# Layer 0 of a four-layer hybrid: the transposed delta comes back from memory, carries and delta u are done for a pair of scans at once, row and column sums are added in memory

## The chip, the cores and the metric

One Trainium2 chip, and of it one core. The time is device microseconds of that core for one execution of the whole program: four layers in a row, of which the change touches only the first. Names used below: PE is TensorE, DVE VectorE, ACT ScalarE, POOL GpSimd, SP the engine whose queue issues most of the DMAs.

## What is computed

Layer 0 is a selective state-space model run over images of 64 x 64 tokens in four scanning orders, with 256 channels and 16 states per channel. There are four images. Cut to what matters:

```
xc, z = split(x @ w_in);  xa = silu(conv3x3(xc) + conv_b)          # depthwise
dts, Bp, Cp = split(xa @ w_xproj);  delta = softplus(dts @ w_dt + b_dt)
xs = [xa by rows, xa by columns, both of these backwards]           # 4 orders
for each order, token i in that order:                              # delta, B, C always by rows
    h[d, n] = h[d, n] * exp(delta[d, i] * A[d, n]) + delta[d, i] * xs[d, i] * B[n, i]
    y[d, i] = sum over n of h[d, n] * C[n, i]
y = the four y put back in row order and added, + 4 * D * xa        # D is added once per order
out = layernorm(y) * silu(z) @ w_out
```

Only xs differs between the four orders; delta, B and C are those of the row order for all of them, so that the decay exp(delta A) is shared.

## The kernel before

**Tiling.** A unit is one image b and one half h of the 256 channels, so there are 8 units. A unit is cut in 64 chunks c of 64 tokens, which makes N = 512 iterations I of one loop. In an iteration the state tile `st` holds, for each of the 4 orders u, 128 partitions (64 channels x 2 halves of the states) by 16 x 64 elements. Orders are taken in two pairs, kp = 0 (u = 0, 1) and kp = 1 (u = 2, 3). Below, a *turn* is the work of one pair in one iteration; there are 1024 turns.

**A turn.** `products` (line 637) makes delta * u * B for two orders with eight matmuls of 64 x 64 x 512 on PE. Each order's result fills one `db` tile of two PSUM banks. The pool of `db` has three buffers, that is six banks, and a turn takes two of them. `scan` then does, for each order, an addition of the carry of the chunk before into the first column of each state (line 650) and the scan itself over 1024 elements (line 653), both on DVE. POOL makes the next carry (line 661) and multiplies the states of the pair by C in place (line 669). `total` sums over the states with matmuls against a stack of two identities (line 682), half of the states per call, into `yp`, and ACT copies the four results to `yr` and `yc`, which hold the row sums and the column sums of a whole unit (line 701). In the later half of the chunks the sums that stand there already are added first by four matmuls with the identity (line 694).

**Delta times u.** The scan's input wants delta with tokens on the partitions. `start` has ACT turn a chunk of delta round (line 599), `delta` transposes it and its mirror image on PE into `pt2` (line 617), and `inputs` multiplies it with the two tiles of u, `xo`, in two DVE operations (line 628). `yp` and `pt2` are halves of one PSUM tile, `aux`, which fills one bank.

**Work beside the loop.** Two steps of a generator run in each iteration, one after each turn: in the h = 0 units `back` (layer norm and output of the image before) and `front` (group norm and w_in of the image after) or, for the first image, `also` (tables for layer 1); in the h = 1 units `middle` (convolution, B, C and delta of the image after). What is left of the steps at chunk 59 of an h = 1 unit is run there at once. This work has one PSUM bank of its own, `bg`. `front` and `middle` of the first image run before the loop and take their banks from the `db` pool (`turn_bank`).

**What sets the order.** Inside the loop PE, DVE and ACT execute in the order in which the Python code records the instructions. POOL and SP are ordered by a scheduler. [...]a wait is a semaphore that another engine raises when an instruction is finished. Which waits are needed is worked out by the framework from the tiles that an instruction reads and writes. The loop body, cut to the calls:

```
nxt = start(I + 1); diagonal(nxt)
bs = products(now, 0); scan(I, now, 0, ...)
total(I - 2, 1); next(beside)
bs = products(now, 1); delta(nxt); inputs(nxt); scan(I, now, 1, ...)
next(beside); total(I - 1, 0)
```

Of the kernel before, what the change touches and what calls it, by code (L numbers as in the profile page):

```python
# [14 lines left out]
P = 128  # L15
# [144 lines left out]
def layer0(cm, x, W, x1, also, kept):  # L160
# [5 lines left out]
    with ExitStack() as ctx:  # L166
# [4 lines left out]
        t4 = ctx.enter_context(tc.tile_pool(name="l0t4", bufs=4))  # L171
        p2 = ctx.enter_context(tc.tile_pool(name="l0p2", bufs=2))
        db = ctx.enter_context(tc.tile_pool(name="l0db", bufs=3, space=PSUM))
# [31 lines left out]

        both = tl(wp, [P, TC], "both")
# [26 lines left out]


        yr = tl(wp, [P, S], "yr")
        yc = tl(wp, [P, S], "yc")

        aux = tl(pp, [P, 2, 2, P], "aux")
        yp = aux[:, 0].rearrange("p k (j t) -> p k j t", t=TC)
        pt2 = aux[:, 1]  # L240
# [19 lines left out]
        def begin(b):  # L260
            img[b] = {
                "zs": tl(dr, [P, 2, S], "zs"),
                "dl": tl(dr, [2, P, S], "dl_d"),
                "ct": tl(dr, [NST, S], "ct_d"),
                "xT": tl(dr, [2, S, P], "xT_d"),
                "y0": tl(dr, [P, 2, S], "y0_d"),
                "yr": tl(dr, [P, 2, S], "yr_d"),
            }
# [77 lines left out]
        def shifted(i, pool, tag):  # L346

            k, h = divmod(i, 2)
            x3 = tl(pool, [3 * CG, 4, 8 * PADW], tag, bufs=None if tag == "big" else 1)
            for dy in range(3):  # L350
                s0 = (8 * k + dy) * PADW
                nc.sync.dma_start(
                    x3[dy * CG : (dy + 1) * CG],
                    xc_d[4 * h : 4 * h + 4, :, s0 : s0 + 8 * PADW].rearrange("g p s -> p g s"),
                )
            return x3

        def middle(b, bank, pool, tag, ahead):

            ready = [shifted(i, pool, tag) for i in range(ahead)]  # L360
            for k in range(NBLK):
                cols = slice(k * BLK, (k + 1) * BLK)
                xa = []
                for h in range(2):
                    ps = bank()
                    x3 = ready.pop(0)
                    for dx in range(3):
                        for g in range(4):
                            nc.tensor.matmul(
                                ps[g * CG : (g + 1) * CG, :], lhsT=cdiag[:, 4 * h + g, dx, :],  # L370
                                rhs=x3[:, g, 0 : 8 * PADW].rearrange(
                                    "p (r w) -> p r w", w=PADW
                                )[:, :, dx : dx + HW],
                                start=(dx == 0), stop=(dx == 2),
                            )
                    if 2 * k + h + ahead < 2 * NBLK:
                        ready.append(shifted(2 * k + h + ahead, pool, tag))
                    xh = tl(tmp, [P, BLK], "t2k")
                    nc.scalar.activation(xh, ps, AF.Silu, bias=vec[:, 0, h : h + 1])
                    y0 = tl(tmp, [P, BLK], "t2k")  # L380
                    nc.scalar.activation(y0, xh, AF.Copy, scale=d4[:, h : h + 1])
                    nc.sync.dma_start(img[b]["y0"][:, h, cols], y0)
                    xa.append(xh)
                    yield
                    ps = bank()
                    for i in range(4):
                        nc.tensor.transpose(
                            ps[:, i * P : (i + 1) * P], xa[h][:, i * P : (i + 1) * P], cm.ident
                        )
                    t = tl(tmp, [P, 4, P], "t2k")  # L390
                    nc.scalar.copy(t, ps.rearrange("p (t c) -> p t c", c=P))
                    nc.sync.dma_start(
                        img[b]["xT"][h, cols, :].rearrange("(t p) c -> p t c", p=P), t
                    )
                    yield
                    if h == 0:
                        yield
                        yield
# [49 lines left out]
                yield  # L448
# [82 lines left out]
        def load(q):  # L531
# [3 lines left out]
            dl = tl(p2, [P, QC * TC], "dl")  # L535
            nc.sync.dma_start(dl, img[b]["dl"][h, :, cols])
# [6 lines left out]
            return {"dl": dl, "dp": dp, "dA": dA[q % 2], "h": h}  # L543
# [21 lines left out]
        def fetch(I):  # L565
# [9 lines left out]
            xo = tl(p2, [P, 2, P], "xo", bufs=3)  # L575
            xT = img[b]["xT"][h]
# [12 lines left out]
            inp[I] = {"ct": ct, "xo": xo, "dg": dg}  # L589
# [4 lines left out]
        def start(I):  # L594
            b, h, c = place(I)
            q = {"c": c, "h": h, "w": quads[I // QC], **inp.pop(I)}
            dlc = q["w"]["dl"][:, c % QC * TC : (c % QC + 1) * TC]
            dlr = tl(p2, [P, TC], "dlr")
            nc.scalar.copy(dlr, dlc[:, ::-1])
            q["dl"] = dlc, dlr  # L600
            return q
# [11 lines left out]
        def delta(q):  # L613

            pt = pt2[:, q["c"] % 2]
            for j in range(2):
                nc.tensor.matmul(  # L617
                    pt[j * TC : (j + 1) * TC, :], lhsT=q["dl"][j], rhs=cm.ident,
                    start=True, stop=True,
                )  # L620
            q["pt"] = pt

        def inputs(q):

            q["du"] = []
            for kp in range(2):
                d_ = tl(p2, [P, P], f"du{kp}")
                nc.vector.tensor_tensor(d_, q["xo"][:, kp, :], q["pt"], ALU.mult)  # L628
                q["du"].append(d_)

        def products(q, kp):
            bs = [tl(db, [P, 2 * NH0, TC], "db") for _ in range(2)]
            for g in range(2):
                for j in range(2):
                    half = slice(j * TC, (j + 1) * TC)
                    for p in range(2):
                        nc.tensor.matmul(  # L637
                            bs[j][p * TC : (p + 1) * TC, g * NH0 : (g + 1) * NH0, :],
                            lhsT=q["du"][kp][half, g * TC : (g + 1) * TC],
                            rhs=q["dg"][half, p * NH0 : (p + 1) * NH0, :],  # L640
                            start=True, stop=True,
                        )
            return bs

        def scan(I, q, kp, bs, st, old, new):
            c = q["c"]
            for j in range(2):
                u = 2 * kp + j
                if c:
                    nc.vector.tensor_tensor(  # L650
                        bs[j][:, :, 0], bs[j][:, :, 0], old[:, u, :], ALU.add
                    )
                nc.vector.tensor_tensor_scan(  # L653
                    st[:, u].rearrange("p n t -> p (n t)"),
                    q["w"]["dA"][:, c % QC].rearrange("p g n t -> p (g n t)"),
                    bs[j].rearrange("p n t -> p (n t)"),
                    0.0, ALU.mult, ALU.add,
                )
            us = slice(2 * kp, 2 * kp + 2)
# [16 lines left out]
        def total(I, part):  # L676
            b, h, c = place(I)
            st = states[I]
            late = c >= NCHUNK // 2
            for n in range(4 * part, 4 * part + 4):  # L680
                for p in range(2):
                    nc.tensor.matmul(  # L682
                        yp[p * TC : (p + 1) * TC], lhsT=both,
                        rhs=st[:, :, p * NH0 + n, :], start=(n == 0),
                        stop=(n == NH0 - 1 and not late),
# [3 lines left out]
            vs = [views(yc if kp else yr, c)[2 * j + kp] for j in range(2) for kp in range(2)]  # L689
            for j in range(2 if late else 0):  # L690

                for kp in range(2):
                    v = vs[2 * j + kp]
                    nc.tensor.matmul(  # L694
                        yp[:, kp, j, :], lhsT=cm.ident, rhs=v[:, ::-1] if j else v,
                        start=False, stop=(j + kp == 2),
                    )
# [5 lines left out]
            if late and c % 8 == 7:  # L703
                for r in (c - 7, NCHUNK - 1 - c):
                    rows = slice(r * TC, (r + 8) * TC)
                    nc.sync.dma_start(img[b]["yr"][:, h, rows], yr[:, rows])
            if c == NCHUNK - 1:
                for r in range(2):
                    rows = slice(r * S // 2, (r + 1) * S // 2)
                    nc.gpsimd.dma_start(  # L710
                        img[b]["y0"][:, h, rows], yc[:, rows], accum_op=ALU.add
                    )

        def turn_bank():
            return tl(db, [P, BLK], "db")
# [8 lines left out]
        for _ in run(front(0, turn_bank), middle(0, turn_bank, big, "big", 2)):  # L724
            pass
        N = 2 * B * NCHUNK
        states, quads, inp = {}, {0: load(0), 1: load(1)}, {}
# [9 lines left out]
        delta(nxt)  # L737
# [10 lines left out]
        with tc.manual_schedule(engines=engines):  # L748
            for I in range(N):
                b, h, c = place(I)  # L750
                clock[0] = I
                if h == 0 and c == 4:
                    gens = [back(b - 1, own_bank) if b else also(
                        tl(p2, [P, 4, 8 * PADW], "x3", bufs=1)[:, 0, 0 : 4 * C], tmp, t4, own_bank
                    )]
                    if b + 1 < B:
                        gens += [
                            front(b + 1, own_bank), wait(I - c + NCHUNK),
                            middle(b + 1, own_bank, p2, "x3", 1),
# [20 lines left out]
                bs = products(now, 0)  # L780
                scan(I, now, 0, bs, st, carry, new)
                if I > 1:
                    total(I - 2, 1)
# [9 lines left out]
                bs = products(now, 1)  # L793
                if nxt:
                    delta(nxt)
                    inputs(nxt)
                scan(I, now, 1, bs, st, carry, new)
                if beside:
                    next(beside, None)
                if I:  # L800
                    total(I - 1, 0)
                carry = new
            total(N - 2, 1)
            total(N - 1, 0)
            total(N - 1, 1)
# [4 lines left out]
def spectra(cm, W, cst, sp_d, room, tmp, t4, bank):  # L810

    nc = cm.nc
    kern = room.rearrange("p (a c) -> p a c", c=C)
# [1504 lines left out]
```

## Time and profile before

| what | value |
|---|---|
| median of 3 executions | 11008.79 us (10986.12 to 11056.8) |
| the profiled execution | 10974.05 us, span 10972.3 us |
| mean granted TensorE clock | 0.898 |
| before the loop (first scan starts) | 281.7 us |
| the loop, first scan to last | 281.7 to 6370.9 us, 6089 us, 11.9 us per iteration |
| its busiest engines, us busy in the loop | PE 5445.6, DVE 5422.5, POOL 5073.8, ACT 3063.3 |

The rest of the span, from 6371 us on, is layers 1 to 3. In the lists, a line such as L653 is line 653 of the kernel before; a group is all instructions of one line and shape, with its busy time, the mean of one in ns, and the idle time of its engine just before. PE's matmuls of 32-bit floats appear as two records each.

### The profile page before, as it was taken

The numbers are of one execution on the slowest core, as the hardware profiler recorded it, in microseconds if no ns is written. First come the engines' busy times: TensorE is split into PE (matmuls) and PEld (weight loads), VectorE is DVE, ScalarE is ACT, GpSimd is POOL, SyncE is SP. The second block draws the span as 40 slices with busy tenths as digits, with TensorE's granted clock in tenths as the row PEclk, the third lists the DMA queues.
The fourth block names the chain that finished last, engine by engine and source line by source line (L and its number), as shares of the span: only waits on it lengthen the run. The fifth ranks groups of instructions, "written<-read, shape, count | busy, mean of one in ns | idle before, by whom it ended". The sixth has DMA issues, their size and how long they took to land. (4 is left out here: it accounts for less than half of the span.)

```text
span 10972.3 us, 163387 instructions
## 1 busy us (share of the span) xinstructions
PE 9474.1 (86%) x59368; PEld 4529.1 (41%) x59368; DVE 7569.2 (69%) x11174; ACT 5425.1 (49%) x13536; POOL 5331.9 (49%) x2581
## 2 busy tenths in 40 slices
PE   6789998889998899998889954999999956988886
PEld 2344444344443344443344432444444434544442
DVE  1898988888988898988899966545452122355546
ACT  6666543555544564545542223777776622433321
POOL 0788888878888888887889940000000000000000
PEclk7899999999999899998999977999999976677777
DMA  5334443334443334443333341111100065022101
GB/s 147 106 107 149 131 128 114 109 109 149 136 132 116 107 117 151 135 122 113 109 106 99 103 120 36 41 35 35 39 24 17 16 191 104 17 46 56 37 24 46
DMA packets 1471160, 1009.46 MB, mean 92 GB/s; under 512 B 697540, under 2 KB 1296296, under 8 KB 1466008
## 3 DMA queue, kind: packets, MB, share of 16 engines
q1 hardware_dynamic: 1468056, 982.24, 30.3%
q0 software_dynamic: 2304, 16.78, 0.7%
q8 instruction: 475, 7.78, 0.3%
q14 instruction: 325, 2.66, 0.1%
HBM read 667.01 MB, written 331.61 MB: 91 GB/s over the span
## 5 line engine op out<-in xcount | busy, mean ns | idle before, releaser
L653 DVE TENSOR_TENSOR_SCAN big<-dA,db 128x1024 f32<-128x1024 f32 x2048 | 4680.0, 2286 | 82.1 <-ACT dA L560 3.2
L669 POOL TENSOR_TENSOR big<-big,ct 128x2048 f32<-128x2048 f32 x1024 | 4646.1, 4537 | 85.0 <-DVE big L653 5.4
L637 PE MATMUL db<-dg,du 64*64 64x512 f32 x16384 | 2442.7, 617 | 101.1 <-DVE db L650 87.8
L682 PE MATMUL aux<-big,both 128*64 128x256 f32 x16384 | 2104.0, 401 | 407.1 <-DVE db L650 260.6
L682 PEld LDWEIGHTS aux<-big,both 128*64 128x64 f32 x16384 | 1202.8, 142 | 1396.1 <-issue 622.9
L701 ACT COPY yr<-aux 128x64 f32<-128x64 f32 x1024 | 226.6, 222 | 2668.6 <-PE aux L694 1250.7
L637 PEld LDWEIGHTS db<-dg,du 64*64 64x64 f32 x16384 | 748.2, 135 | 1321.2 <-issue 1218.4
L608 ACT ACTIVATE dg<-mask,BT 128x64 f32<-128x64 f32 x4096 | 1007.4, 341 | 4.0 <-DMA dg_d<-dg 4.0
L1441 PE MATMUL av<-e,x 128*128 128x512 f32 x2048 | 974.0, 592 | 4.6 <-ACT e L1436 4.6
L1392 PE MATMUL qk<-a,xT 128*128 128x512 f32 x2048 | 966.6, 594 | 8.6 <-ACT e L1396 7.8
L1396 ACT ACTIVATE e<-qk,nk 128x512 f32<-128x512 f32 x1024 | 692.9, 685 | 539.2 <-PE qk L1392 538.4
L560 ACT ACTIVATE dA<-dp,A 128x252 f32<-128x252 f32 x2048 | 870.5, 509 | 1.4
L971 POOL TENSOR_TENSOR g_rs<-g_rs,qrow 128x4 f32<-128x4 f32 x32 | 41.1, 1285 | 1499.9 <-DVE g_rs L970 1499.9
L661 POOL TENSOR_TENSOR cy<-big,a 128x32 f32<-128x32 f32 x1008 | 272.8, 271 | 821.7 <-DVE big L653 524.4
L1392 PEld LDWEIGHTS qk<-a,xT 128*128 128x128 f32 x2048 | 378.0, 190 | 462.3 <-issue 358.0
L1441 PEld LDWEIGHTS av<-e,x 128*128 128x128 f32 x2048 | 381.6, 190 | 434.7 <-issue 393.6
L1436 ACT ACTIVATE e<-e 128x1024 f32<-128x1024 f32 x510 | 538.7, 1056 | 15.3
L1917 ACT ACTIVATE e<-s 72x576 f32<-72x576 f32 x448 | 273.3, 642 | 492.0 <-PE s L1910 489.0
L628 DVE TENSOR_TENSOR du<-xo,aux 128x128 f32<-128x128 f32 x1024 | 248.2, 284 | 379.5 <-PE aux L617 286.2
L650 DVE TENSOR_TENSOR db<-db,cy 128x16 f32<-128x16 f32 x2016 | 336.9, 167 | 202.0 <-PE db L637 184.2
L1928 POOL COPY vp<-vt 72x160 f32<-72x160 f32 x56 | 19.6, 352 | 890.8 <-PE po L1934 874.4
L2150 DVE SCALAR_TENSOR_TENSOR tex<-x,gw,tex 128x128 f32<-128x128 f32 x768 | 264.5, 344 | 256.1 <-PE x L2144 241.2
(525 smaller groups left out, 10869.4 us busy)
## 6 DMA issues: line engine op xcount, KB each, us to landing
ct<-ct_d SPq DMA_DIRECT2D x1024, 128.0 KB
dg_d<-dg SPq DMA_DIRECT2D x256, 512.0 KB
dg<-dg_d SPq DMA_DIRECT2D x256, 512.0 KB
xo<-xT_d SPq DMA_DIRECT2D x2048, 32.0 KB
x<-xc_d SPq DMA_DIRECT2D x144, 264.0 KB
dp<-dl_d SPq DMA_DIRECT2D x256, 128.0 KB
t2k<-in_x SPq DMA_DIRECT2D x96, 256.0 KB
sp<-sp_d SPq DMA_DIRECT2D x16, 1280.0 KB
```

The lines of the kernel that those rows point to most:

```text
L560: nc.scalar.activation(w["dA"][:, :, g, n, 1:], w["dp"][:, g, :, 1:], AF.Exp, scale=A[:, w["h"], g, n : n + 1],)
L608: nc.scalar.activation(q["dg"][:, n, :], mask, AF.Copy, scale=BT[:, q["c"], n : n + 1])
L637: nc.tensor.matmul(bs[j][p * TC : (p + 1) * TC, g * NH0 : (g + 1) * NH0, :], lhsT=q["du"][kp][half, g * TC : (g + 1) * TC], rhs=q["dg"][ha ...
L650: nc.vector.tensor_tensor(bs[j][:, :, 0], bs[j][:, :, 0], old[:, u, :], ALU.add)
L653: nc.vector.tensor_tensor_scan(st[:, u].rearrange("p n t -> p (n t)"), q["w"]["dA"][:, c % QC].rearrange("p g n t -> p (g n t)"), bs[j].re ...
L669: nc.gpsimd.tensor_tensor(sv, sv, q["ct"].rearrange("p n t -> p (n t)").unsqueeze(1) .to_broadcast([P, 4, NH0 * TC]), ALU.mult,)
L682: nc.tensor.matmul(yp[p * TC : (p + 1) * TC], lhsT=both, rhs=st[:, :, p * NH0 + n, :], start=(n == 0), stop=(n == NH0 - 1 and not late),)
L1392: nc.tensor.matmul(ps, lhsT=me["xT"][:, kt * P : (kt + 1) * P], rhs=me["a"][k], start=True, stop=True,)
L1396: nc.scalar.activation(e[:, j, :], ps, AF.Exp, bias=me["nk"][:, kt : kt + 1], scale=2.0)
L1436: nc.scalar.activation(es[g + 2], es[g + 2], AF.Exp)
L1441: nc.tensor.matmul(avs[b, k], lhsT=img[b]["x"][:, kt, :], rhs=e[:, j, :], start=(kt == 0), stop=(kt == NT - 1),)
L1917: nc.scalar.activation(e.rearrange("p j h q -> p j (h q)"), ss[p][0:HALF, :, 0 : 2 * WIN], AF.Exp, scale=0.5,)
```

## The change

- Delta is stored transposed too: `middle` transposes it, copies it, mirrors it by one matmul with a matrix `flip`, and writes both to `dT` in memory. `fetch` loads a chunk of it as `dt`. `delta`, the mirrored copy in `start`, and the loads of `dl` are gone. `inputs` is one operation on 128 x 256 elements instead of two on 128 x 128.
- `db` is no longer a pool of three tiles but one tile of three slots. `turns` lists which two slots a turn takes and in which order they are scanned. The carries of both orders are added by one operation, ahead of both scans. `turn_bank` gives slices of the same tile.
- The row sums of eight chunks and the column sums of half a unit are kept in pairs of small tiles `ys`. The later half is added to the earlier by DMAs that accumulate in memory, issued by POOL, instead of by matmuls.
- Both parts of `total` come one step later: part 0 of I - 2 after the first turn, part 1 of I - 2 after the second.
- `middle` has 15 steps per block of 512 tokens instead of 12; the loads of `shifted` are split in two, and use the tiles of `back`.

The diff, cut to its core:

```diff
-        db = ctx.enter_context(tc.tile_pool(name="l0db", bufs=3, space=PSUM))
+        db = tl(pp, [P, 3, 2 * NH0, TC], "db")
-        yr = tl(wp, [P, S], "yr")
-        yc = tl(wp, [P, S], "yc")
-        aux = tl(pp, [P, 2, 2, P], "aux")
-        yp = aux[:, 0].rearrange("p k (j t) -> p k j t", t=TC)
-        pt2 = aux[:, 1]
+        yp = tl(pp, [P, 2, 2, TC], "yp")
...
         (middle)
-                    if h == 0:
-                        yield
-                        yield
...
                     nc.sync.dma_start(img[b]["dl"][h, :, cols], r)
-                yield
+                    yield
+                    ps = bank()
+                    for i in range(4):
+                        nc.tensor.transpose(
+                            ps[:, i * P : (i + 1) * P], r[:, i * P : (i + 1) * P], cm.ident
+                        )
+                    for j in range(2):
+                        t = tl(tmp, [P, 4, P], "t2k")
+                        nc.scalar.copy(t, ps.rearrange("p (t c) -> p t c", c=P))
+                        nc.sync.dma_start(
+                            img[b]["dT"][h, j, cols, :].rearrange("(t p) c -> p t c", p=P), t
+                        )
+                        yield
+                        if j == 0:
+                            ps = bank()
+                            nc.tensor.matmul(
+                                ps, lhsT=flip, rhs=t.rearrange("p t c -> p (t c)"),
+                                start=True, stop=True,
+                            )
...
         (fetch)
+            dt = tl(p2, [P, P], "dt", bufs=3)
+            nc.sync.dma_start(dt[0:TC], img[b]["dT"][h, 0, c * TC : (c + 1) * TC, :])
+            nc.sync.dma_start(dt[TC:P], img[b]["dT"][h, 1, c * TC : (c + 1) * TC, :])
...
         def inputs(q):
-            for kp in range(2):
-                d_ = tl(p2, [P, P], f"du{kp}")
-                nc.vector.tensor_tensor(d_, q["xo"][:, kp, :], q["pt"], ALU.mult)
+            q["du"] = tl(p2, [P, 2, P], "du")
+            nc.vector.tensor_tensor(
+                q["du"], q["xo"], q["dt"].unsqueeze(1).to_broadcast([P, 2, P]), ALU.mult
+            )
+        turns = (
+            ({0: 0, 1: 1}, (0, 1), db[:, 0:2]), ({0: 0, 1: 2}, (1, 0), db[:, 0::2]),
+            ({0: 1, 1: 2}, (0, 1), db[:, 1:3]),
+        )
-        def products(q, kp):
-            bs = [tl(db, [P, 2 * NH0, TC], "db") for _ in range(2)]
+        def products(q, kp, turn):
+            bs = turn[0]
...
-                            bs[j][p * TC : (p + 1) * TC, g * NH0 : (g + 1) * NH0, :],
+                            db[p * TC : (p + 1) * TC, bs[j], g * NH0 : (g + 1) * NH0, :],
...
         (scan)
-            for j in range(2):
-                u = 2 * kp + j
-                if c:
-                    nc.vector.tensor_tensor(
-                        bs[j][:, :, 0], bs[j][:, :, 0], old[:, u, :], ALU.add
-                    )
+            if c:
+                nc.vector.tensor_tensor(
+                    turn[2][:, :, :, 0], turn[2][:, :, :, 0], old[:, us, :], ALU.add
+                )
+            for j in turn[1]:
                 nc.vector.tensor_tensor_scan(
...
         (total)
-            for j in range(2 if late else 0):
-                for kp in range(2):
-                    v = vs[2 * j + kp]
-                    nc.tensor.matmul(
-                        yp[:, kp, j, :], lhsT=cm.ident, rhs=v[:, ::-1] if j else v,
-                        start=False, stop=(j + kp == 2),
-                    )
...
+            if r == 7:
+                for i, r0 in enumerate((c - 7, NCHUNK - 1 - c)):
+                    to = img[b]["yr"][:, h, r0 * TC : (r0 + 8) * TC]
+                    if c < NCHUNK // 2:
+                        nc.sync.dma_start(to, ys[i])
+                    else:
+                        nc.gpsimd.dma_start(to, ys[i], accum_op=ALU.add)
+            if c % (NCHUNK // 2) == NCHUNK // 2 - 1:
                 for r in range(2):
                     nc.gpsimd.dma_start(img[b]["y0"][:, h, rows], ..., accum_op=ALU.add)
+        banks = [0]
         def turn_bank():
-            return tl(db, [P, BLK], "db")
+            banks[0] += 1
+            return db.rearrange("p u n t -> p (u n t)")[
+                :, banks[0] % 6 * BLK : (banks[0] % 6 + 1) * BLK
+            ]
...
-                bs = products(now, 0)
-                scan(I, now, 0, bs, st, carry, new)
+                turn = turns[2 * I % 3]
+                products(now, 0, turn)
+                scan(I, now, 0, turn, st, carry, new)
                 if I > 1:
-                    total(I - 2, 1)
+                    total(I - 2, 0)
...
-                bs = products(now, 1)
+                turn = turns[(2 * I + 1) % 3]
+                products(now, 1, turn)
                 if nxt:
-                    delta(nxt)
                     inputs(nxt)
-                scan(I, now, 1, bs, st, carry, new)
+                scan(I, now, 1, turn, st, carry, new)
...
-                if I:
-                    total(I - 1, 0)
+                if I > 1:
+                    total(I - 2, 1)
```

## The prediction

> **What bounds the kernel now.** First the busy time by stretch. The columns are the stretch, its length, and busy us of PE, weight loads, DVE, ACT and POOL, then granted clock, DMA share and GB/s. The first row is the loop, the second 40 iterations of the last unit, where no step runs beside the loop.
>
> ```profile
> 281.70:6370.90 6089.20, 5445.57 (x40140) 2533.47 (x40140) 5422.50 (x5481) 3063.29 (x9878) 5073.81 (x2345) 0.95 0.39 120
> 5836.00:6248.00 412.00, 381.64 (x2868) 178.58 (x2868) 398.69 (x402) 92.06 (x370) 386.67 (x181) 1.00 0.34 102
> ```
>
> In the quiet stretch DVE is busy 398.69 of 412 us, 97%: an iteration is 10.3 us there, and is four scans and their small operations. The groups of the page give their lengths (mean ns after the busy time):
>
> ```profile
> L653 DVE TENSOR_TENSOR_SCAN big<-dA,db 128x1024 f32<-128x1024 f32 x2048 | 4680.0, 2286 | 82.1 <-ACT dA L560 3.2
> L669 POOL TENSOR_TENSOR big<-big,ct 128x2048 f32<-128x2048 f32 x1024 | 4646.1, 4537 | 85.0 <-DVE big L653 5.4
> L637 PE MATMUL db<-dg,du 64*64 64x512 f32 x16384 | 2442.7, 617 | 101.1 <-DVE db L650 87.8
> ```
>
> How DVE reaches 97% is seen in the timeline of the quiet stretch (start, length, engine, line):
>
> ```profile
> 5856.90 2.29 DVE L653 TENSOR_TENSOR_SCAN big<-dA,db 128x1024 f32<-128x1024 f32 x1
> ...
> 5858.27 2.99 PE L637 MATMUL db<-dg,du 64*64 64x512 f32 x16
> ...
> 5859.10 0.16 DVE L650 TENSOR_TENSOR db<-db,cy 128x16 f32<-128x16 f32 x1
> 5859.30 2.29 DVE L653 TENSOR_TENSOR_SCAN big<-dA,db 128x1024 f32<-128x1024 f32 x1
> 5859.30 0.24 PEld L637 LDWEIGHTS db<-dg,du 64*64 64x64 f32 x8 [0.83 <-issue]
> ```
>
> The first scan of a turn ends at 5859.19. At 5859.30 PE resumes the products of the next turn, in the slot just freed, while DVE makes the second scan. **Products of one turn lie beside the second scan of the turn before.** Without that, DVE waits for them. The trace shows such a case, at 2024, where PE was late; PE and then DVE:
>
> ```profile
> 2022.23 3.34 PE L682 MATMUL aux<-big,both 128*64 128x256 f32 x16 [3.37 <-POOL big L669]
> 2025.50 1.95 PE L637 MATMUL db<-dg,du 64*64 64x512 f32 x16
> 2027.38 1.95 PE L682 MATMUL aux<-big,both 128*64 128x256 f32 x16
> ```
>
> ```profile
> 2021.98 2.29 DVE L653 TENSOR_TENSOR_SCAN big<-dA,db 128x1024 f32<-128x1024 f32 x1
> 2027.55 0.18 DVE L650 TENSOR_TENSOR db<-db,cy 128x16 f32<-128x16 f32 x1 [3.29 <-PE db L637]
> 2027.77 2.29 DVE L653 TENSOR_TENSOR_SCAN big<-dA,db 128x1024 f32<-128x1024 f32 x1
> ```
>
> From the first product matmul to the carry's addition it is 2.05 us, and 0.22 us more to the scan.
>
> [...]`total` on PE starts at 5862.40, only after DVE has read the other half of the same bank, `aux` (L628, until 5862.25). [...]the recorded clock changes in steps of 3.41 us, and the 16 records of L682 take 1.95 us at most places and 3.3 to 3.7 us after a gap, as at 2022.23 after 3.37 us. [...]it is POOL that issues `y_d<-yc`; a pair of these held POOL up by some 2 us at 1067.
>
> **The change, part by part.**
>
> *The new wait.* I resolved the semaphore counts in the built instructions of both kernels. In before, the third product matmul of a turn waits for the count raised by the first scan of the turn ahead, the first matmul for an older one. In the changed kernel the first product matmul waits for the second scan of the turn ahead, in all 1018 turns that have a DVE wait: the first scan of a pair raises nothing, the second raises by two. `turns` avoids the slot, but one tile is tracked as one thing. So no product starts beside a scan, and each turn is a chain:
>
> - first scan to the start of the second, 2.20 (scan to next DVE start, 5856.90 to 5859.10; at most 2.29);
> - second scan to its end, 2.29;
> - scan end to first matmul, 0.14 (5859.19 to the weight load at 5859.30, and 0.03);
> - products and their signal, 2.05 (at 2025.50);
> - addition of both carries, 0.22 to the scan (as at 2027.55; it has 32 elements for 16, I add nothing).
>
> Sum 6.90 us, 13.80 per iteration against 10.3 in the quiet stretch and 11.9 on average. 1024 turns are **7066 us**.
>
> *What it removes.* Two DVE additions (0.2 each) are in that sum. The two delta multiplications (0.48 together), `delta` and the four matmuls of L694 on PE (0.65 and 1.15 us), the mirrored copy on ACT: worth nothing, because DVE idles 2.2 us per turn and PE 2.8. The new 128 x 256 multiplication is not in the trace: between 0.28, one of today's, and 0.66, today's 128 x 512 addition L512. Either fits into the 2.2 us. If that cover were gone it would cost itself.
>
> *The later `total`.* It follows the products on PE and ends 4.1 us into a turn of 6.90. Its waits for POOL, and for DVE in the shared bank, go; what is late next is the products, so no gain. Waits of ACT for `yc` and `yr` at unit starts (up to 21 us) go too, and are not in the 7066.
>
> *Clock.* A turn has PE busy 4.1 us, idle 2.8. In this trace nearly every window with less than a third of busy time was followed by half clock. The idle stretch is long enough for that in about half of all phases against two windows (6.83 us), and a hit lengthens the products by some 1.4 us (3.34 against 1.95). But a hit also fills the next window and shifts the phase, and work beside the loop fills gaps. Bounds 0 and 0.7 per turn; I take 0.15, **+154**.
>
> *Work beside the loop.* On PE a turn has room for 2.6 us; only the convolution (2.78) exceeds it, 48 times by 0.3, **+14**. On DVE there is room for 2.2 us: the step of `back` with the reciprocal (3.33 + 1.28) exceeds it by 2.4 and brings a cold turn (1.3), 24 times, **+89**; that of the spectra (1.7 + 3.5) by 3.0, 8 times, **+34**. POOL, 9.7 of 13.8 us per iteration, takes 12 accumulating DMAs a unit at 1 us each without loss. At unit starts its wait for fetched sums remains: **+10**. SP issues for 7.7 us of an iteration now; two loads of `dt` add 1.2, which fits in 13.8. A DMA queued ahead of `xo` has an iteration and a half of lead.
>
> *Steps left over.* In units 3 and 5, `back` and `front` take 140 steps of the 118 of the h = 0 unit; 96 remain for the 120 of `middle` (before: 96 for 96). In the built order, two blocks' DVE work stands together at chunk 59. These 24 steps run one after the other through the bank `bg`, about 75 us, 70 of them uncovered: **+140**.
>
> *Before the loop.* `turn_bank` is now the same tile: in the built program each group of matmuls waits for the reader of the bank ahead. Rows of the stretch ahead of the loop:
>
> ```profile
> L369 PE MATMUL db<-big,cdiag 96*32 96x512 f32 x384 | 71.4, 900 | 3.2 <-DMA big<-xc_d 3.2
> L387 PE MATMUL db<-ident,t2k 128*128 128x128 f32 x64 | 14.6, 369 | 49.6 <-ACT t2k L379 49.6
> ```
>
> So 4.46 us per convolution (71.4/16), 0.91 per four transposes. A block of `middle` in series: convolution 4.46 and silu 0.69, transposes 0.91 and copy 0.58, twice, 13.3; w_xproj and its copies 3.3; B 1.95; delta 9.4 (matmul 1.42, five ACT operations, two table loads of 1.28, three DVE of 0.70), its transposes and copy 1.5, mirror and copy 1.8, twice, 25.4; some 24 handovers at 0.11. That is 46.5 us against 25.8 now ((278.5 - 71.9)/8): +165. A block of `front` goes from 5.06 to 8.9: +30. Together **+195**.
>
> Sum: the loop 7066 + 154 + 14 + 89 + 34 + 10 + 140 = 7507 against 6089, +1418; before it +195. The profiled execution had 10974, so 12,587; the median lies 35 above it, **12,620**.
>
> **The rivals.** *PE follows the first scan after all*, as the slots of `turns` would allow. DVE then needs 2 x (2.20 + 2.20 + 0.22) + 0.35 = 9.6 us and POOL 2 x 4.84 + 0.12 + 0.19 = 10.0 an iteration: 0.3 less in quiet stretches, up to 0.65 elsewhere (some 260), 16 us less at each of 7 unit starts, and +28 ahead of the loop: 10,665, **faster**. It decides as soon as the products are done before the second scan ends. For it: the slots in use never overlap, and DVE is 97% busy today. Against: the counts in the program. *The clock stays low*: every turn's products take 3.4 us. Then 1024 x 1.25 more, 13,900. For it: 2.8 us idle in 6.9. Against: the threshold seen needs more idle time in most phases.
>
> **Chances.** Main case 0.82; low clock 0.12; the faster rival 0.04; the rest spread. Range from clock 0, half the surcharges and +100 ahead of the loop (12,250) to clock +0.6 and +260 there (13,150). About 1% is what a measurement of this kernel can tell from no change. Faster 0.04, within 1% 0.01, slower 0.95.
>
> **What would show it.** In the profile after: every first carry addition waits about 2.2 us for PE's products; scans come in pairs 2.2 us apart and turns 6.9; DVE falls to about 75% in the loop, POOL to 70%; the first scan starts near 475 us; two gaps of 70 us stand late in units 3 and 5. Wrong would be: product matmuls during a scan, or products of 3.4 us throughout.

## The result, and the profile after

The changed kernel takes 12,926 us (median of 4 executions, 12,903 to 12,964), the kernel before beside it 11,017 us: a ratio of 1.173, interval 1.169 to 1.178. The profiled execution, at 12,964 us with a span of 12,962.3, is the slowest of the four. Its time by stretch, in the columns of the table ahead of the prediction (first the part ahead of the loop, then the loop, then 640 us of the last unit):

```profile
0.00:533.40 533.40, 291.24 (x1012) 101.61 (x1012) 46.54 (x97) 218.99 (x360) 1.59 (x10) 0.70 0.34 99
533.40:8321.40 7788.00, 5100.31 (x36336) 2038.96 (x36338) 5482.34 (x3962) 3027.86 (x9421) 5186.92 (x2423) 0.91 0.36 103
7560.00:8200.00 640.00, 365.66 (x2976) 148.87 (x2976) 446.57 (x325) 101.83 (x380) 459.47 (x215) 0.98 0.31 85
```

The loop went from 6089 to 7788 us, the stretch ahead of it from 281.7 to 533.4. In the quiet stretch DVE is busy 446.57 of 640 us, 70% for 97% before; no engine is near full. The groups of the page (busy time, mean ns, then idle time before them and its releaser):

```profile
L684 POOL TENSOR_TENSOR big<-big,ct 128x2048 f32<-128x2048 f32 x1024 | 4653.7, 4545 | 108.8 <-DVE big L669 19.6
L669 DVE TENSOR_TENSOR_SCAN big<-dA,db 128x1024 f32<-128x1024 f32 x2048 | 4571.7, 2273 | 85.2 <-PE db L654 40.5
L654 PE MATMUL db<-dg,du 64*64 64x512 f32 x16384 | 2363.7, 699 | 2565.2 <-DVE big L669 2476.0
...
L665 DVE TENSOR_TENSOR db<-db,cy 128x32 f32<-128x32 f32 x1008 | 200.3, 199 | 2095.5 <-PE db L654 2014.6
...
L637 DVE TENSOR_TENSOR du<-xo,dt 128x256 f32<-128x256 f32 x512 | 434.0, 848 | 17.6 <-DMA xo<-xT_d 17.5
```

Scans and multiplications are as long as before. PE's idle time ahead of the products rose from 101 to 2565 us, nearly all of it ended by the scan (L669), and DVE's ahead of the carry's addition is 2095 us, ended by the products: each waits for the other. The timeline of the quiet stretch shows the handover, DVE first, then PE:

```profile
8057.43 0.20 DVE L665 TENSOR_TENSOR db<-db,cy 128x32 f32<-128x32 f32 x1 [2.13 <-PE db L654]
8057.67 4.46 DVE L669 TENSOR_TENSOR_SCAN big<-dA,db 128x1024 f32<-128x1024 f32 x2
8062.05 0.40 DVE L637 TENSOR_TENSOR du<-xo,dt 128x256 f32<-128x256 f32 x1
8064.26 0.20 DVE L665 TENSOR_TENSOR db<-db,cy 128x32 f32<-128x32 f32 x1 [1.81 <-PE db L654]
```

```profile
8055.36 1.95 PE L654 MATMUL db<-dg,du 64*64 64x512 f32 x16 [3.00 <-DVE big L669]
8057.24 1.95 PE L704 MATMUL yp<-big,both 128*64 128x256 f32 x16
8062.19 1.95 PE L654 MATMUL db<-dg,du 64*64 64x512 f32 x16 [3.00 <-DVE big L669]
```

Both scans run from 8057.67 to 8062.13; the products start at 8062.19, not at the end of the first scan. A turn is 6.83 us, an iteration 13.67 for 10.28. In none of the 1023 turns that follow another do products start earlier than 0.05 us after the second scan.

One thing was not foreseen: the group of `du` has a mean of 848 ns. Most of its 512 operations take 0.40 us, but 60 take over 2 us, up to 4.75. Such a place, on DVE, POOL and PE:

```profile
2798.65 0.66 DVE L533 TENSOR_TENSOR t2k<-t2k,bg 128x512 f32<-128x512 f32 x1
2799.23 4.74 DVE L637 TENSOR_TENSOR du<-xo,dt 128x256 f32<-128x256 f32 x1
2803.89 0.19 DVE L665 TENSOR_TENSOR db<-db,cy 128x32 f32<-128x32 f32 x1
```

```profile
2798.81 0.26 POOL L676 TENSOR_TENSOR cy<-big,a 128x32 f32<-128x32 f32 x1 [2.01 <-DVE big L669]
2799.15 4.52 POOL L684 TENSOR_TENSOR big<-big,ct 128x2048 f32<-128x2048 f32 x1
```

```profile
2798.78 1.95 PE L654 MATMUL db<-dg,du 64*64 64x512 f32 x16 [1.01 <-DVE big L669]
...
2808.72 3.69 PE L654 MATMUL db<-dg,du 64*64 64x512 f32 x16 [6.11 <-ACT dA L579]
```

`du` ends 0.3 us after POOL's multiplication does; so do all 59 that take over 2.1 us, 0.28 or 0.29 us after one. The one that begins clearly first goes first: of the 79 `du` that begin while a multiplication runs, the 73 that come 0.07 us or more after its start end only after it. The six that come within 0.02 us of its start take 0.41 us, and the multiplication then takes 4.8 us for 4.5. In the place shown the products were ready at 2800.7, and the turn lost some 3 us; the idle PE then made the next products at the lower clock (3.69 us; the recorded clock is a half from 2807.08 to 2813.90). The step beside the loop (L533) had pushed `du` behind the start of POOL's multiplication.

### The profile page after: what moved, and what is told of

It reads as the page before. It is cut to its first block, busy times and chain, and to the rows that moved or that the text cites. A ratio compares the mean times of both kernels' runs of the same rounds, so it can differ in the third digit from the quotient of the medians.

```text
span 12962.3 us, 154646 instructions
## 1 busy us (share of the span) xinstructions
PE 9275.5 (72%) x55656; PEld 4089.7 (32%) x55656; DVE 7635.0 (59%) x9657; ACT 5420.5 (42%) x13148; POOL 5438.7 (42%) x2661
## 5 line engine op out<-in xcount | busy, mean ns | idle before, releaser
L669 DVE TENSOR_TENSOR_SCAN big<-dA,db 128x1024 f32<-128x1024 f32 x2048 | 4571.7, 2273 | 85.2 <-PE db L654 40.5
L654 PE MATMUL db<-dg,du 64*64 64x512 f32 x16384 | 2363.7, 699 | 2565.2 <-DVE big L669 2476.0
L704 PE MATMUL yp<-big,both 128*64 128x256 f32 x16384 | 2133.1, 405 | 26.1 <-ACT yc L718 22.1
L654 PEld LDWEIGHTS db<-dg,du 64*64 64x64 f32 x16384 | 600.8, 147 | 3748.2 <-DVE big L669 2282.3
L704 PEld LDWEIGHTS yp<-big,both 128*64 128x64 f32 x16384 | 1151.8, 145 | 1450.3 <-issue 1029.5
L676 POOL TENSOR_TENSOR cy<-big,a 128x32 f32<-128x32 f32 x1008 | 312.4, 310 | 2739.8 <-DVE big L669 2309.2
L665 DVE TENSOR_TENSOR db<-db,cy 128x32 f32<-128x32 f32 x1008 | 200.3, 199 | 2095.5 <-PE db L654 2014.6
L718 ACT COPY yr<-yp 128x64 f32<-128x64 f32 x1024 | 225.4, 221 | 2495.0 <-PE yp L704 2494.5
L637 DVE TENSOR_TENSOR du<-xo,dt 128x256 f32<-128x256 f32 x512 | 434.0, 848 | 17.6 <-DMA xo<-xT_d 17.5
```

Source lines behind the costliest of these rows:

```text
L637: nc.vector.tensor_tensor(q["du"], q["xo"], q["dt"].unsqueeze(1).to_broadcast([P, 2, P]), ALU.mult)
L654: nc.tensor.matmul(db[p * TC : (p + 1) * TC, bs[j], g * NH0 : (g + 1) * NH0, :], lhsT=q["du"][half, kp, g * TC : (g + 1) * TC], rhs=q["dg" ...
L669: nc.vector.tensor_tensor_scan(st[:, 2 * kp + j].rearrange("p n t -> p (n t)"), q["w"]["dA"][:, c % QC].rearrange("p g n t -> p (g n t)"), ...
L704: nc.tensor.matmul(yp[p * TC : (p + 1) * TC], lhsT=both, rhs=st[:, :, p * NH0 + n, :], start=(n == 0), stop=(n == NH0 - 1),)
```

## The experiments

**The tile.** e1_pool gives `db` back its pool of three tiles:

```diff
-        db = tl(pp, [P, 3, 2 * NH0, TC], "db")
+        db = ctx.enter_context(tc.tile_pool(name="l0db", bufs=3, space=PSUM))
...
+            bs = [tl(db, [P, 2 * NH0, TC], "db") for _ in range(2)]
...
-                    turn[2][:, :, :, 0], turn[2][:, :, :, 0], old[:, us, :], ALU.add
+                    bs[j][:, :, 0], bs[j][:, :, 0], old[:, 2 * kp + j, :], ALU.add
```

> The changed kernel with db as a pool of three tiles again (and so one carry addition per order, and separate tiles for the stretch ahead of the loop); all else as changed. Theory A, the single tile makes the first product wait for the second scan: the first product follows the first scan again, a quiet iteration takes 10.0 to 10.8 us instead of 13.67, the first scan starts near 310 us instead of 533, in all 10,650 to 11,250 us. Theory B, something else in the change (the later total, the accumulating DMAs, the load of dt) makes the turn long: a quiet iteration stays above 13 us and the time above 12,500.

11,392 us, 1.037 (1.035 to 1.039) of the kernel before. PE's wait ahead of the products falls from 2565 to 582 us; groups of the page:

```profile
L649 PE MATMUL db<-dg,du 64*64 64x512 f32 x16384 | 2801.4, 647 | 581.5 <-DVE db L662 448.5
...
L637 DVE TENSOR_TENSOR du<-xo,dt 128x256 f32<-128x256 f32 x512 | 540.0, 1055 | 24.1 <-DMA dg<-dg_d 14.9
```

and the products lie beside the second scan again (timeline, DVE, then PE):

```profile
6056.85 2.29 DVE L665 TENSOR_TENSOR_SCAN big<-dA,db 128x1024 f32<-128x1024 f32 x1
6059.05 0.16 DVE L662 TENSOR_TENSOR db<-db,cy 128x16 f32<-128x16 f32 x1
```

```profile
6058.16 3.06 PE L649 MATMUL db<-dg,du 64*64 64x512 f32 x16
```

A quiet iteration takes 10.1 us. Theory A holds for the turn; the time is above its range, because `du` is held up even more (1055 ns on average) and the first scan starts at 414 us, not 310. That leaves open whether the paired addition, which this run takes back too, shares in the wait; e4_two_adds below answers it.

e2_one_tile puts the tile alone into the kernel before, with the `turns` and the paired addition of the change.

> The kernel before with only db made one tile of three slots and the carries of a pair added in one operation. Theory A: turns of 6.9 us as in the changed kernel, and the bank wait ahead of the loop, so 12,300 to 12,900 us. Theory B, the rest of the change does it: within 2% of the kernel before, 10,900 to 11,250.

13,039 us, 1.187 (1.185 to 1.189): above theory A's range, and the tile with its paired addition costs more than the whole change. Beside the turn of 6.83 it has one that is longer, since delta is still transposed on PE between products and `du` (DVE, then PE):

```profile
8000.51 4.46 DVE L658 TENSOR_TENSOR_SCAN big<-dA,db 128x1024 f32<-128x1024 f32 x2
8007.45 0.48 DVE L628 TENSOR_TENSOR du<-xo,aux 128x128 f32<-128x128 f32 x2 [2.48 <-issue]
8007.85 0.19 DVE L653 TENSOR_TENSOR db<-db,cy 128x32 f32<-128x32 f32 x1
```

```profile
8005.03 1.95 PE L642 MATMUL db<-dg,du 64*64 64x512 f32 x16 [1.15 <-DVE big L658]
8006.91 0.32 PE L617 MATMUL aux<-ident,dl 128*64 128x128 f32 x1
```

The products end at 8006.98; 0.47 us with the transposition and 0.40 with `du` follow on the path before the carry's addition.

e4_two_adds keeps the tile and takes only the paired addition back:

```diff
-            if c:
-                nc.vector.tensor_tensor(turn[2][:, :, :, 0], turn[2][:, :, :, 0], old[:, us, :], ALU.add)
             for j in turn[1]:
+                if c:
+                    nc.vector.tensor_tensor(
+                        db[:, turn[0][j], :, 0], db[:, turn[0][j], :, 0], old[:, 2 * kp + j, :], ALU.add)
```

> The changed kernel with the one tile kept, but one carry addition per order, each just ahead of its scan. Theory A, the tile is the cause: the wait stays, one addition more lies on the chain, 12,900 to 13,150 us. Theory E, the addition over both slots ties the pair together: products follow the first scan again, under 11,500.

13,541 us, 1.233 (1.231 to 1.235). Not the paired addition but the tile makes the wait. The size was missed: the pair of scans takes 4.82 us for 4.46, so that the shortest turn is 7.17, and the products are at the low clock (the eight of a turn take over 2.6 us for 1.95) in 456 turns, for 237 in the changed kernel. PE, in a stretch without work beside the loop:

```profile
8061.09 1.95 PE L654 MATMUL db<-dg,du 64*64 64x512 f32 x16 [3.41 <-DVE big L670]
8062.97 1.95 PE L705 MATMUL yp<-big,both 128*64 128x256 f32 x16
8068.26 2.42 PE L654 MATMUL db<-dg,du 64*64 64x512 f32 x16 [3.34 <-DVE big L670]
8070.61 3.11 PE L705 MATMUL yp<-big,both 128*64 128x256 f32 x16
8075.89 3.22 PE L654 MATMUL db<-dg,du 64*64 64x512 f32 x16 [2.16 <-DVE big L670]
```

**The hold-up of `du`.** e3_du_first moves one line of the changed kernel:

```diff
                 scan(I, now, 0, turn, st, carry, new)
+                if nxt:
+                    inputs(nxt)
                 if I > 1:
                     total(I - 2, 0)
...
                 products(now, 1, turn)
-                if nxt:
-                    inputs(nxt)
```

> The changed kernel with the multiplication by delta u recorded directly after the first pair of scans, ahead of the step beside the loop. Theory C, the long du operations (3.3 to 4.75 us) are those that meet a POOL multiplication already running, since both inputs now come from SBUF: du runs ahead of the multiplication, stays at 0.40 us, and 150 to 200 us go: 12,720 to 12,800 us. Theory D, they wait for a load (dt or xo): asked for earlier, du waits at least as long, and the time stays at 12,900 or rises.

12,688 us, 1.155 (1.153 to 1.157), 0.019 of the kernel before (205 us) less than the changed kernel by the ratios, 238 by the medians. Its group:

```profile
L637 DVE TENSOR_TENSOR du<-xo,dt 128x256 f32<-128x256 f32 x512 | 230.1, 450 | 17.3 <-DMA xo<-xT_d 17.3
```

The loads were not the cause, since an earlier `du` does not wait for them. The gain was above the range: 129 us less between products and scan, and another 108 less in products at the low clock (175 for 237).

e5_pool_psum is e1_pool with one input of `du` in PSUM:

```diff
+            q["pt"] = aux[:, 1, c % 2]
+            nc.scalar.copy(q["pt"], q["dt"])
...
-                q["du"], q["xo"], q["dt"].unsqueeze(1).to_broadcast([P, 2, P]), ALU.mult
+                q["du"], q["xo"], q["pt"].unsqueeze(1).to_broadcast([P, 2, P]), ALU.mult
```

> The changed kernel with db as a pool again (as e1_pool) and, beside that, ACT copies the loaded dt to PSUM, from where du's multiplication reads it, so that only one of its inputs is in SBUF. Theory C, DVE and POOL exclude each other where a DVE operation has both inputs in SBUF: du falls from a mean of 1.06 us to about 0.45, the 335 us that it was held up in e1_pool mostly go, 11,000 to 11,150 us. Theory F, POOL bounds e1_pool anyway and the hold-up of du costs nothing: 11,330 to 11,420 us, as e1_pool.

11,149 us, 1.013 (1.012 to 1.015), and in its groups:

```profile
L641 DVE TENSOR_TENSOR du<-xo,aux 128x256 f32<-128x256 f32 x512 | 204.0, 398 | 19.3 <-PE aux L704 11.8 <-DMA dl_d<-t2k 7.6
```

The same operation beside the same multiplications is not held up in this run, where one input comes from PSUM: 381 of the 512 overlap a multiplication, 176 of them begin and end inside one, and the longest takes 0.42 us. In the changed kernel, with both inputs in SBUF, all 73 `du` that begin 0.07 us or more after a multiplication end only after it, and take up to 4.75 us behind a multiplication of 4.5. What in the chip makes the one wait for the other is not shown.

**The clock.** e8_warm adds work to PE that changes no sum:

```diff
+                for i in range(6 if n % 4 == 0 else 0):
+                    p = i % 2
+                    nc.tensor.matmul(
+                        yp[p * TC : (p + 1) * TC], lhsT=zero,
+                        rhs=st[:, :, p * NH0 + n, :], start=False, stop=False,
+                    )
```

> The changed kernel with six more matmuls with zero weights in each half of total (they add zeros to yp), so that PE is busy about 5.5 us of a turn instead of 4.1. Theory G, products of 3.3 to 3.7 us come from the clock falling after idle windows: nearly all products take 1.95 us, and of the 370 us above 1.95 at least 300 go: 12,520 to 12,650 us. Theory H, these products are long for another reason (weights or inputs late): their number stays, and the time is 12,900 us or, with more work on PE, above.

12,830 us, 1.166 (1.164 to 1.168). The products at the low clock fell from 237 to 95, and their time above 1.95 us from 368 to 158 us, so theory G holds: PE's idle time ahead of the products is 1450 us for 2565, and fewer of them are slow. The time is above its range all the same, since only some 80 to 96 us were gained: the work added on PE made products late elsewhere (62 us more after the second scan, 34 more ahead of the carry).

**The steps left over.** e6_extra runs one step more in odd chunks of the h = 1 units:

```diff
-                if beside:
-                    next(beside, None)
+                for _ in range(1 + (h == 1 and c % 2 == 1)):
+                    if beside:
+                        next(beside, None)
```

> The changed kernel with one step beside the loop more in each odd chunk of the h = 1 units, so that none is left over at chunk 59. Theory I, the two gaps of about 75 us at chunk 59 of units 3 and 5 are steps run alone that would otherwise lie beside the turns: 100 to 150 us go, 12,780 to 12,830 us. Theory J, a turn has no room for a third step, and they cost the same wherever they run: 12,880 to 12,960 us.

12,817 us, 1.165 (1.163 to 1.167). In the changed kernel the iterations ahead of chunk 59 of units 3 and 5 take 91.3 and 90.2 us; here 13.6. The waits inside the first of these gaps show that its steps run in series, each engine waiting for the next:

```profile
DVE bg L444 <- ACT t2k L442: 37.9, 4, 12.6
PEld bg L454 <- DVE t2k L448: 35.9, 4, 9.7
PE bg L454 <- DVE t2k L448: 31.0, 4, 8.1
```

About two thirds of the two gaps' 153 us are won.

e7_pool_psum_extra joins this with e5_pool_psum.

> e5_pool_psum with the extra steps of e6_extra. If the single tile, the hold-up of du and the steps left over are all that counts, what remains against the kernel before is the longer stretch ahead of the loop (399 us against 282) less what the rest of the change gains: 149 us over before less 100 to 150 from the two gaps, 10,990 to 11,050 us. If something else of the change costs time in the loop, it stays above 11,080.

11,105 us, 1.010 (1.008 to 1.011), above both marks. Yet its loop runs from 400.8 to 6491 us, 6090 us, and that of the kernel before 6089: over the whole loop gains and losses cancel, and the 119 us ahead of it are left. By units they do not: units 2, 4 and 6 (h = 0) take 771, 773 and 745 us for 811, 807 and 791 in the kernel before, and units 1, 3 and 5 (h = 1, with `middle` beside them) 778, 803 and 788 for 747, 746 and 750. So something else of the change does cost time, in the h = 1 units, as much as the change gains in the others; b2_sums_late below, with neither the tile nor the loaded delta, shows the same pattern. Taking the two gaps away won 44 us here by the medians, 109 in the changed kernel; that the added steps have less room in turns of 5 us than in those of 6.8 is likely, but was not shown.

**Sums in memory alone.** b1_sums takes only `ys` and the accumulating DMAs from the change, and the tiles for the convolution's loads.

> Of the change only the row and column sums added in memory (pairs of small tiles, accumulating DMAs by POOL), with the tiles for the convolution that go with it; db, delta, du and the order of total as before. Theory K, the waits of ACT for the sums at unit starts and the late additions on PE go: 60 to 150 us faster than before, 10,840 to 10,930 us. Theory L, POOL, with 9.67 of 10.3 us per iteration busy in quiet stretches, pays some 1 us for each of the 96 accumulating DMAs, which takes the gain back: within 0.5% of before, or slower.

10,921 us, 0.993 (0.992 to 0.995): faster than both kernels, within theory K's range. Gone are the waits for the sums at unit starts, which the list of ACT's waits of the kernel before gives in the loop (us, times, longest):

```profile
ACT yr L701 <- DMA yr_d<-yr: 69.7, 6, 21.0
ACT yc L701 <- DMA y_d<-yc: 66.6, 6, 16.7
```

In the profiled execution (10,960 us) the loop falls by 59 us, to 6030, and the stretches ahead of it and after it are 24 and 22 us longer. POOL's DMAs did not take the gain back. How much of it comes from these waits, and how much from the additions on PE that are gone too, was not separated.

b2_sums_late adds the later `total`, b3_sums_late_early an earlier mirrored copy.

> b1_sums with both parts of total one step later, as in the change (and, so that the bank shared with delta is free, the transposition of delta ahead of the first products and du ahead of the first scan). Theory M, in the h = 0 units PE waits in total for POOL's multiplication and so brings the next products late (those units took 806 us in b1_sums, and 761 in e5_pool_psum, where total comes later): 100 to 200 us faster than b1_sums, 10,720 to 10,830 us. Theory N, the difference of these units comes from the delta that is loaded transposed: within 0.5% of b1_sums.

11,010 us, 1.001 (1.000 to 1.002). Neither theory is right. The later `total`, or the earlier delta and `du` that came with it, does help where M said: units 2, 4 and 6 take 775, 768 and 746 us for 806, 804 and 792, and a quiet iteration 9.99 for 10.28. But units 1, 3 and 5 rise from 730, 742 and 730 us to 781, 792 and 802, and unit 0 from 765 to 805.

> b2_sums_late with ACT's mirrored copy of delta recorded at the end of the iteration before, so that the transposition of delta, now at the head of PE's iteration, does not wait for ACT. Theory O, in b2_sums_late the units with work on ACT (780 to 805 us for the h = 1 units, against 730 to 742 in b1_sums) lost time because delta, and behind it the products, waited for ACT's queue: these units come to 730 to 750 us and the whole to 10,760 to 10,880. Theory P, their loss has another cause: 10,970 to 11,030 us, as b2_sums_late.

11,000 us, 1.001 (1.000 to 1.002), and units 1, 3 and 5 at 781, 795 and 803: theory O falls. In the list of waits of unit 3 it is not the mirrored copy that PE waits for ahead of the transposition, but ACT's copies of the sums, which stand in the same tile `aux`:

```profile
PEld aux L617 <- ACT yc L702: 90.2, 62, 5.0
```

That these waits cost the 50 to 70 us of a unit is not shown, and whether a tile of its own would mend it was not tried. Why the h = 1 units lose stays open.

## Why the prediction was right, and where its sizes were off

The likeliest case came true, and its mechanism was the one given: the single tile, read in the built instructions, and shown by e1_pool, e2_one_tile and e4_two_adds. (That `total` starts at 5862.40, after the other half of `aux` is read at 5862.25, does not tell a bank from a tile, since `aux` is both.) The measured median is 306 us above the forecast, within the range. The turns came out a little shorter than forecast, every other row longer; the largest miss is the clock, 214 us, half of which goes with the hold-up of `du`. The sizes were thus right within the range and not term by term. Against the profiled execution, step by step (measured times by summing the parts of all 1023 turns: scan pair, end of scan to products, products, products to scan; each counted above the length that a tenth of the turns stay under). The sums put these rows in place of the 6089 us of the loop within the 10,974 us of the kernel before:

| step | predicted, us | measured, us |
|---|---|---|
| ahead of the loop | +195 | +252 (`front` 66, `middle` 185) |
| turns, without surcharges | 7066 | 6968 (1023 x 6.81) |
| products at the low clock | 154 | 368 |
| products late after work on PE, and the steps left over | 14 + 140 | 191, of it 2 x 76 at chunk 59 |
| DVE late, and unit starts | 89 + 34 + 10 | 255 |
| after the loop | 0 | +40 |
| sum | 12,587 | 12,964 |

- **The turn** was right to 0.1 us. The two ends of it that I had taken from before were each a little long (2.20 and 0.14 for the scans' spacing and the restart; measured 2.17 and 0.05).
- **"The new 128 x 256 multiplication ... Either fits into the 2.2 us"** is the step that failed. The duration was right (0.40 us), the cover was not: it was priced alone, from an operation of before with one input in PSUM, and not against POOL. By the trace 204 of the 255 us of the line "DVE late" fall in turns where `du` was the last DVE operation ahead of the carry (some of them behind a long step that I had counted). By e3_du_first all of it, with the cold products that follow, is worth 205 to 238 us.
- **The clock** came out at 0.36 us per turn for 0.15, inside the bounds of 0 and 0.7. Some of it hangs on the hold-up: 108 us went with it in e3_du_first. In the quiet last unit it is nearly nothing, 6 of 128 turns. The reading behind it was right: in the loop of before all 98 windows of 3.41 us with PE busy under a third were followed by half clock, and 76 of the 1686 others. What was missing was how often a turn meets such a window (the last section).
- **The steps left over** were right in place and size (70 us each forecast, 76 measured).
- **Ahead of the loop** the sum was 57 short, most of it in `front` (66 for 30). e1_pool splits the 252: without the single tile 133 stay, 129 of them in `middle`, where the transposition of delta is new; 119 are the tile's.
- **"Worth nothing"** for the parts removed is wrong as a statement on the parts, though it didn't enter the sum. In e2_one_tile, where they stay in a serial turn, the time is 113 us higher than with the whole change, though it has no hold-up of `du` (longest 0.29 us). Added to the kernel before alone, the sums in memory gain 0.7%.
- **The faster rival** (10,665) had the right iteration, 10.0 us (e1_pool 10.1, e5_pool_psum 9.94), but not the rest: even with the wait gone the changed kernel is 3.7% slower than before. It left out the hold-up (243 us from e1_pool to e5_pool_psum), the gaps at chunk 59, and most of the longer stretch ahead of the loop. The rival with a low clock throughout is out: most products take 1.95 us.
- What was to be seen in the profile came as said: the wait of 2.1 us ahead of the carry's addition (2.2 said), DVE at 70% in the loop and in the quiet stretch (75 said), POOL at 67% (70), the two late gaps. The first scan starts at 533 us, not near 475. The 40 us after the loop lie in layers that the change does not touch; the stretch takes 4641 us here, 4601 before and 4585 to 4637 in the other runs, and I have no cause for the spread.

## What to carry to other kernels

In these kernels the tile is the unit of waiting: slots that never overlap are still one thing if they are slices of one tile, and two engines that worked side by side on separate tiles then work in series (PE's idle time ahead of the products is 2565 us with the one tile and 582 in e1_pool). So when buffers are merged to join two small operations, compare what the joined operation saves (0.36 us a turn, by e4_two_adds) with the overlap that the separate tiles carried (DVE now waits 2.1 us a turn). And when an input of a DVE operation moves from PSUM to SBUF, as that of `du` did here (a mean of 1055 ns in e1_pool, 398 in e5_pool_psum), price it against what POOL is doing at that moment, not by its own length alone.

## What the runs showed of the hardware that I had not expected

- A DVE multiplication of 0.40 us, `du`, took up to 4.75 us while POOL's multiplication of 4.5 us ran; with one input in PSUM its mean is 0.398 us and its longest 0.42 (e5_pool_psum). In the changed kernel the six that began up to 0.02 us after the multiplication still went first (0.41 us), and the multiplication took 4.8 us; the 73 that began 0.07 us or more after it ended only after it.
- The recorded clock of the changed kernel takes two values, full and half, and changes on a grid of 3.41 us; a window is one step of it. In the loop all 276 windows in which PE was busy under four tenths were followed by half clock, and 1877 of the 2006 others by the full clock. Of these 276, 109 had PE busy for three to four tenths, and 76 under a hundredth.
- How often PE fell to the low clock went with how the turn stood to the window in two kernels. The quiet turn of the changed kernel, 6.825 us, is two windows, so that it keeps its place: with PE idle 3.0 us in each turn, 6 of the 128 turns of the last unit have slow products. In e4_two_adds a turn is 7.17 us, with PE idle 3.34, and 54 of 128 do. It goes with the place more than with the 0.3 us more of idle time: of the products that start between 0.1 and 0.6 of a window, none of 118 are slow in the changed kernel and 3 of 64 in e4_two_adds; of those that start elsewhere, 6 of 10 and 51 of 64.
